# A two-layer gated cross-attention block with a mixture of experts: later token groups summed inside the expert loop, and the first steps of layer 0 issued in another order

## The chip, the cores and the metric

The kernel runs on one core of one Trainium2 chip, in one launch. The metric is the device time of the launch in microseconds. The kernel before takes 2547.64 us, the median of three runs (2542.3 to 2548.95).

## The reference

All tensors are float32. `x` is 32 groups of 112 tokens of 256 numbers; `ctx_512` is 32 contexts of 375 rows of 128. Four residual branches follow each other:

```
x = x + tanh(g_xattn[0]) * L0_xattn(layernorm(x), ctx_512)   # 16 heads of 16
x = x + tanh(g_ffn[0])   * L0_ffn(layernorm(x))              # gated recurrence over the 32 groups
x = x + tanh(g_xattn[1]) * L1_xattn(layernorm(x), ctx_512)   # 16 heads of 64
x = x + tanh(g_ffn[1])   * L1_ffn(layernorm(x))              # experts
```

The last one is the branch that most of the change is about:

```
xf = x.reshape(T, D)                                  # 3584 tokens
shared = silu(xf @ Ws_up) @ Ws_down
aff = xf @ centroids.T
_, idx = jax.lax.top_k(aff + expert_biases, 8)        # 8 of 64 experts
w = sigmoid(take_along_axis(aff, idx, axis=1))
w = w / (sum(w, axis=-1) + 1e-08)
...
y = einsum('etf,efd->etd', silu(einsum('td,edf->etf', xf, W_up)), W_down)
routed = sum over the 8 experts of a token of w * y
return shared + routed
```

## The kernel before

A group is one index `b` of 0 to 31, 112 tokens on 112 partitions. The tiles `xs[0]` to `xs[7]` hold four groups each. The kernel has these stages, by the time of the profile: layer 0's attention (0 to about 580 us), the recurrence and layer 1's attention (to about 1990 us), and the experts (to the end).

**The start of layer 0.** Five queues are filled from the first microsecond. SP's queue loads `cols` (L83), `cent` (the centroids, L129), `rows` (all row constants, spread over 112 partitions, L150), `xs[0]` (L331), `cts[0]` (four contexts, L334), `wv` and `wo`. ACT's queue loads `wk` and `wq` and then computes `tg = tanh(gates)` out of `rows` (L151). GpSimd clears buffers, makes `bias0` out of `rows` and `tg` (L397), and raises the variances to the power of minus one half (L402, L405) for the first normalisation; between these two it halves `sdn`, the shared experts' second matrix (L747). VectorE normalises (L411), TensorE turns the result over (L423) and projects queries (`queries0`, L433) and keys (`keys0`, L450). Each projection is copied to SBUF by ACT and then spread by eight small DMAs: a key tile `k` goes into two tiles `kT` (L457, SP's queue), a query tile `q` into `qp` (L441). Before the loop, the eight DMAs of query half 0 are issued by ACT, those of half 1 by SP. Item `n` of the loop (`n // 4` the group, `n % 4` a set of four heads) needs `kT` of item `n` and one four-head part of `qp`: items 0 and 1 use the two parts of half 0, items 2 and 3 those of half 1. `quad` computes the scores `sc` (L483) and their maxima `nm` (L487); two items later the transposed scores `st` (L498) and their exponentials (L504). The call `keys0(n + 2)` stands in every even item, so that the keys of items 2 and 3 are made in item 0. The order of TensorE, VectorE, ACT and GpSimd is the program's own here (a manual schedule).

**The experts.** Each expert's token rows lie in the DRAM table `xrows`. The function `run` works through pairs `n` of 128-row blocks: pairs 0 to 63 are the first two blocks of each expert, the 68 pairs after them (`NSURE` = 136 blocks) are blocks that an expert has beyond 256 rows, ordered by the group in which the block begins. A pair is loaded by SP (L1126), turned over, multiplied up, through silu, down, and scattered by GpSimd's indirect DMAs into the DRAM table `yrows` (L1212), one row for each of a token's 8 experts. A token's branch is the sum of its 8 rows in `yrows`.

**The sums.** There are three forms.

- `early_sums`, groups 0 to 15 (`NHALF` = 16): inside `run`, a group's rows are loaded in two halves of four rows.
- `late_sums`, groups 16 to 20 (up to `NEARLY` = 21): inside `run` from pair `hi - 4` on, two steps to a group, a group's rows loaded in four quarters of two rows (`yq`, 224 KB each) into the five buffers that the blocks `xblk` use. Step 0 of a group adds the pair of quarters that the former group's step 0 loaded, and loads quarters 0 and 1; step 1 does the same for quarters 2 and 3, joins the two halves and adds the sum to `xs` (`to_x`). A quarter takes the next buffer that an addition frees, so that each load but the first of a group waits for an addition of the group before.
- `sums`, groups 21 to 31: after `run`, a group's 8 rows are loaded whole (`y8`, 896 KB), four buffers, with VectorE (L1341, L1346, L1347) and GpSimd (L1342) adding.

Loads in the first two forms are made by `early`: such a load waits for scatters, but not for the newest six (`2 * LAG`). That is right only if no row of the group is in these; so the kernel counts blocks on the chip: `planned` is 6 blocks for each group, and `late` marks a group by whose end more blocks have begun than planned. If one of the first `NEARLY` groups is marked, the program takes a branch in which `run` makes no sums at all, and `sums(0, NEARLY)` follows. By the reference's routing of these inputs, 0 to 98 blocks have begun by the ends of groups 0 to 27, and 129 by the end of group 31; no group is marked.

Between `run` and `sums` stand three branches that every engine takes, for the two forms of `run` (L1355 to L1357), for blocks beyond the sure ones (L1360) and for `sums(0, NEARLY)` (L1365). Each branch that skips code waits for the queues' semaphores and fetches the instructions behind it. Finished groups go to the output two at a time from ACT's queue (`results_out`, L1326).

Of the kernel before, what the change touches and what calls it, by code (L numbers as in the profile page):

```python
# [33 lines left out]
AF = mybir.ActivationFunctionType  # L34
ALU = mybir.AluOpType
# [4 lines left out]
B, S, D = 32, 112, 256  # L40
# [10 lines left out]

NBLK = 216
SBLK = 2 * E
NEARLY = 21
NHALF = 16
EARLY = 8
LAG = 3
NSURE = 136
# [10 lines left out]
R_BO0, R_BOF, R_BO1, R_EB, R_G = 0, 256, 512, 768, 832  # L69
# [4 lines left out]
def flamingo_kernel(ctx: ExitStack, tc: tile.TileContext, a: dict, out: bass.AP):  # L74
    nc = tc.nc
# [8 lines left out]
    tg = const.tile([S, 4], F32, tag="tg", name="tg")  # L84
# [29 lines left out]
    nc.gpsimd.iota(planned32, [[0, 1]], base=2 * (EARLY - 5 - LAG), channel_multiplier=6)  # L114
    planned = rtp.tile([B, 1], F32, tag="planned", name="planned")
    nc.vector.tensor_copy(planned, planned32)
    place32 = rtp.tile([S, TOPK], I32, tag="place32", name="place32")
    nc.gpsimd.iota(place32, [[1, TOPK]], base=0, channel_multiplier=TOPK)
    place = rtp.tile([S, TOPK], F32, tag="place", name="place")
# [6 lines left out]
    half = rtp.tile([S, G], F32, tag="half", name="half")  # L126
    nc.gpsimd.memset(half, -0.5)
    cent = rtp.tile([128, 2, E], F32, tag="cent", name="cent")
    nc.sync.dma_start(cent, a["centT"].rearrange("(c p) e -> p c e", p=128))  # L129
    dram = ctx.enter_context(tc.tile_pool(name="dram", bufs=1, space=DRAM))  # L130
    xrows = dram.tile([E * NT, PW], F32, tag="xrows", name="xrows")
    yrows = dram.tile([NT * TOPK, D], F32, tag="yrows", name="yrows")
# [1 line left out]
    def disjoint(group, ins):  # L134
# [9 lines left out]
    sdn = rtp.tile([F, D], F32, tag="sdn", name="sdn")  # L144
    nc.gpsimd.dma_start(sdn, a["ws_down"])
    attention = ExitStack()
    rows = attention.enter_context(tc.tile_pool(name="rows", bufs=1)).tile(
        [S, NROW], F32, tag="rows", name="rows"
    )
    nc.sync.dma_start(rows, a["rows"].partition_broadcast(S))  # L150
    nc.scalar.activation(tg, rows[:, R_G : R_G + 4], AF.Tanh)  # L151
    work = attention.enter_context(tc.tile_pool(name="work", bufs=2))


# [155 lines left out]
    with ExitStack() as att:  # L310
# [14 lines left out]
        with ExitStack() as ph:  # L325
# [6 lines left out]
            nc.scalar.dma_start(wk, a["wk0"])  # L332
            nc.scalar.dma_start(wq, a["wq0"].rearrange("(c p) m -> p c m", p=128))
            nc.sync.dma_start(cts[0], a["ctxT"][:, 0:G, :])  # L334
            nc.sync.dma_start(wv, a["wv0"])
            nc.sync.dma_start(wo, a["wo0"].rearrange("(c p) m -> p c m", p=128))


            one = wp.tile([128, 1], F32, tag="one", name="one0")
# [40 lines left out]
            def inputs(n):  # L380


                b, g = n // 4, n % 4
                if n == 1:
                    nc.gpsimd.dma_start(xs[1], a["x"][G : 2 * G].rearrange("b s d -> s b d"))
                if g == 2 and b + G < B:
                    nc.gpsimd.dma_start(
                        cts[b // G + 1][:, b % G, :], a["ctxT"][:, b + G, :]
                    )
                if g == 3 and b + 2 * G < B:  # L390
                    nc.gpsimd.dma_start(xs[b // G + 2][:, b % G, :], a["x"][b + 2 * G])
                if g == 0 and 8 <= b < 24 and b % 2 == 0:
                    nc.gpsimd.dma_start(*halves[b // 2 - 4])
# [32 lines left out]
                    )  # L426
                nc.scalar.copy(xTs[g][:, c, :], pt)

            def queries0(g, i, queue=nc.sync):

                pq = ps_m.tile([128, GT], F32, tag="mm", name=f"pq0_{g}_{i}")
                for k in range(2):
                    nc.tensor.matmul(  # L433
                        pq, wq[:, k, 128 * i : 128 * i + 128], xTs[g][:, k, :],
                        start=(k == 0), stop=(k == 1),
                    )

                q = kvp.tile([128, GT], F32, tag="q", name=f"q0_{g}_{i}")
                nc.scalar.activation(q, pq, AF.Identity, bias=bq4[:, i : i + 1], scale=0.25)
                for h in range(8):  # L440
                    queue.dma_start(  # L441
                        qps[g % 2][h % 4 * 32 : h % 4 * 32 + 16, 2 * i + h // 4, :],
                        q[16 * h : 16 * h + 16, :],
                    )

            def keys0(n):

                b, i = n // 4, n % 4 // 2
                pk = ps_m.tile([128, LKV], F32, tag="mm", name=f"pk0_{n}")
                nc.tensor.matmul(  # L450
                    pk, wk[:, 128 * i : 128 * i + 128], cts[b // G][:, b % G, :],
                    start=True, stop=True,
                )
                k = kvp.tile([128, LKV], F32, tag="k", name=f"k0_{n}")
                nc.scalar.activation(k, pk, AF.Identity, bias=cols[:, C_BK + i : C_BK + i + 1])
                for h in range(8):
                    nc.sync.dma_start(  # L457
                        kTs[(n + h // 4) % 6][h % 4 * 32 : h % 4 * 32 + 16, :],
                        k[16 * h : 16 * h + 16, :],
                    )  # L460
# [120 lines left out]
            for j in range(G):  # L581
                normed0(0, j, nc.vector)
            keys0(0)
            for c in range(2):
                turned0(0, c)
            for i in range(2):
                queries0(0, i, (nc.scalar, nc.sync)[i])


            rest = []  # L590
            for n in range(4 * B + 7):
                b, g = n // 4, n % 4
                ng, turn = b // G + 1, (b % G, g)
                inputs(n)
                if ng < NG and b % G == 2:
                    normed0(ng, g)
                quad(n, (0, 1), n - 2, (2, 3))
                for r in rest:
                    r()
                rest = []  # L600
                if ng < NG and turn == (1, 3):
                    row_stats(ng * G + 2)
                if 0 <= n - 3 < 4 * B:
                    values_of(n - 3)
                if 0 <= n - 1 < 4 * B:
                    with_max(n - 1)
                quad(n, (2, 3), n - 2, (0, 1))
                if ng < NG and b % G == 1 and g != 2:
                    row_stats(ng * G + g)
                    if g == 3:  # L610
                        rstd0(ng)
                if g == 2 and b >= 2:
                    row_stats(b - 2)
                    if (b - 2) % G == G - 1:
                        inverse_std(rstd_r, (b - 2) // G)
                if n % 2 == 0 and n + 2 < 4 * B:
                    keys0(n + 2)
                if b < B and g < NKC:
                    values0(b, g)
                if ng < NG and turn in ((2, 3), (3, 0)):  # L620
                    turned0(ng, (g + 1) % 4)
                if ng < NG and turn in ((3, 1), (3, 2)):
                    queries0(ng, g - 1, nc.gpsimd)
                if g == 3 and b >= 1:
                    rest.append(divided(b - 1))
                elif g == 0 and b >= 2:
                    rest.append(turned_back(b - 2))
                elif g == 1 and b >= 2:
                    rest.append(output0(b - 2))
# [12 lines left out]
        with ExitStack() as ph:  # L642
# [79 lines left out]
            for t in range(B):  # L722
# [6 lines left out]
                h = work.tile([S, D], F32, tag="t", name=f"h_{t}")  # L729
# [11 lines left out]
        with ExitStack() as ph:  # L741
# [2 lines left out]
            ps_s = ph.enter_context(tc.tile_pool(name="ps_s1", bufs=4, space=PSUM))  # L744
            ps_m = ph.enter_context(tc.tile_pool(name="ps_m1", bufs=3, space=PSUM))
            ps_o = ph.enter_context(tc.tile_pool(name="ps_o1", bufs=1, space=PSUM))
            nc.gpsimd.tensor_scalar(sdn, sdn, 0.5, None, ALU.mult)  # L747
            rstd = rstd_1
            xns, xTs, qTs, kTs, vs, ps, pTs, outs, pos = ({} for _ in range(9))
            routing = []  # L750
# [181 lines left out]
            for n in range(N + 3):  # L932
# [14 lines left out]
                h, c = n // 8 + 1, n % 8  # L947
                g, i = n // 16 + 1, n % 16
# [52 lines left out]
    with tc.tile_pool(name="tables", bufs=1) as ep:  # L1001
# [24 lines left out]
        for k, (lhs, rhs) in enumerate((  # L1026
# [19 lines left out]
        nc.tensor.matmul(  # L1046
            pt[:, 1:2], late[:NEARLY], ones[:NEARLY, 0:1], start=True, stop=True
        )
# [223 lines left out]
    def late_sums(t):  # L1272
# [3 lines left out]
        if t >= 2:  # L1276
# [4 lines left out]
            if k:  # L1281
                add(z, live["q", c, 1])
                to_x(c, z)
                if c % 2 and c < NEARLY:
                    results_out(c - 1)
        if b < NEARLY:
            for q in (2 * k, 2 * k + 1):
# [5 lines left out]
    def run(lo, hi, with_sums=False):  # L1293
        with tc.manual_schedule(engines={
            nc.tensor.engine, nc.vector.engine, nc.scalar.engine, nc.sync.engine,
        }):
            for n in range(lo, min(lo + 4, hi)):
                rows_in(n)
            for n in range(lo, hi + 7 + with_sums):
                if n + 4 < hi:  # L1300
                    rows_in(n + 4)
                if n % 8 == 0 and n < 48:
                    weights(2 + n // 8, nc.sync)
                if n < hi:
                    turned(n)
                if lo <= n - 2 < hi:
                    up(n - 2)
                if lo <= n - 4 < hi:
                    if n - 4 < E:
                        down(n - 4)  # L1310
                    else:
                        hidden_turned(n - 4)
                if lo <= n - 6 < hi and E <= n - 6:
                    down(n - 6)
                if with_sums and n >= E + EARLY:
                    early_sums(n - E - EARLY)
                if with_sums and n >= hi - 4:
                    late_sums(n - hi + 4)
# [46 lines left out]
    with tc.If(is_late > 0):  # L1365
        sums(0, NEARLY)
    sums(NEARLY, B)

# [56 lines left out]
```

## Time and profile before

| what | value |
|---|---|
| median of the runs | 2547.64 us (2542.3 to 2548.95) |
| time of the profiled execution | 2544.75 us |
| its span | 2543.0 us |
| busy share of the span: TensorE, VectorE, ACT, GpSimd | 91%, 66%, 47%, 36% |
| first two score matmuls of item 2 of layer 0 | 36.19 us |
| granted TensorE clock, 28 to 44 us | 0.50 |
| last quarter-wise sum ends | 2481.16 us |
| first whole-group load issued, first one added | 2488.12 us, 2495.99 us |
| last whole-group load added | 2535.62 us |

The profile is of one execution. A line of the timeline has the start and the duration in microseconds, the engine (a name with q is an engine's queue: register work, branches, semaphores and DMA issues), the line of the source, the operation with output and inputs, and in brackets how long the engine had been idle and what ended that. A DMA's line is its issue, not its transfer; when it has landed is seen from who waited for it. A line of the window view has, for each stretch, the busy time of the engines, the granted clock, the mean busy share of the 16 DMA engines and what they moved in GB/s.

### The profile page before, as it was taken

Reading aid. Unit: us, or ns where it says so; the run is one execution under the profiler, and the core shown is the slowest. Engines: PE = TensorE matmul, PEld = TensorE weight load, DVE = VectorE, ACT = ScalarE, POOL = GpSimd, SP = SyncE. Lnnn points to the kernel's source line nnn. Section 1 sums busy time; section 2 is a strip of 40 time slices with the busy share of each in tenths; the row PEclk is TensorE's granted clock in tenths of the full one; section 3 lists DMA queues with packets and bytes.
Section 4 is the critical chain, followed back from the end, with each engine's and each line's share of the span. In section 5 each row is a group of like instructions: output and inputs, shape, how many; then the busy total and the mean of one; then the engine's idle time right before and its main releaser. Section 6 shows DMA issues by size and latency. Waiting matters only on the chain. (4 is left out here: it accounts for less than half of the span.)

```text
span 2543.0 us, 64448 instructions
## 1 busy us (share of the span) xinstructions
PE 2303.5 (91%) x24199; PEld 1811.8 (71%) x24199; DVE 1685.7 (66%) x5075; ACT 1190.8 (47%) x3156; POOL 910.0 (36%) x1149
## 2 busy tenths in 40 slices
PE   7999999999999999999999999999999487888860
PEld 4777777778996777777777777777777366666640
DVE  5666666764327778777777877777777544455565
ACT  2555555543334555555555555555555143344430
POOL 3333333201000034333334443443344466655552
PEclk8999999999999999999999999999999698899985
DMA  3122211116300000000000000000101687567777
GB/s 84 50 57 64 60 49 50 38 34 223 118 1 1 2 26 29 27 29 27 29 29 30 29 29 29 29 28 27 31 29 33 204 277 236 166 201 223 207 202 182
DMA packets 144313, 204.56 MB, mean 80 GB/s; under 512 B 26168, under 2 KB 120970, under 8 KB 143985
## 3 DMA queue, kind: packets, MB, share of 16 engines
q1 hardware_dynamic: 101040, 99.80, 14.0%
q0 software_dynamic: 36352, 94.05, 11.4%
q10 hardware_dynamic: 6592, 6.39, 0.8%
q8 instruction: 199, 3.26, 0.5%
q14 instruction: 130, 1.06, 0.1%
HBM read 100.67 MB, written 88.74 MB: 74 GB/s over the span
## 5 line engine op out<-in xcount | busy, mean ns | idle before, releaser
L301 POOL DMA_INDIRECT xrows<-row,at x256 | 256.1, 1001 | 530.0 <-DVE at L298 340.3
L841 ACT ACTIVATE p_a<-ps_a,nmax_a 112x375 f32<-112x375 f32 x512 | 286.2, 571 | 232.2 <-DVE nmax_a L840 156.5
L487 DVE TENSOR_REDUCE nm<-sc 112x1 f32<-112x375 f32 x512 | 256.7, 543 | 182.5 <-PE st L498 138.5
L1212 POOL DMA_INDIRECT yrows<-yblk,dst x264 | 261.7, 991 | 208.5 <-ACT yblk L1200 121.0
L504 ACT ACTIVATE pT<-st 125x336 f32<-125x336 f32 x512 | 202.7, 448 | 252.8 <-PE st L498 252.8
L865 PEld LDWEIGHTS pt_a<-ident,p_a 112*125 112x125 f32 x1536 | 224.4, 188 | 78.7 <-ACT v L819 19.2
L840 DVE TENSOR_REDUCE nmax_a<-ps_a 112x1 f32<-112x375 f32 x512 | 244.4, 539 | 20.0 <-PE ps_a L836 17.2
L483 PE MATMUL sc<-kT,qp 32*112 32x375 f32 x1024 | 233.3, 526 | 3.1 <-DMA qp<-q 1.8
L498 PE MATMUL st<-qa,kT 32*125 32x112 f32 x3072 | 234.8, 284 | 0.0
L865 PE MATMUL pt_a<-ident,p_a 112*125 112x112 f32 x1536 | 228.3, 271 | 0.6 <-ACT kT L801 0.6
L812 PE MATMUL pv<-wv,c 128*125 128x256 f32 x768 | 216.3, 391 | 10.3 <-ACT kT L801 6.2
L797 PE MATMUL pk<-c,wk 128*128 128x375 f32 x512 | 208.0, 488 | 4.1
L890 PEld LDWEIGHTS pav<-pT_a,v 64*64 64x64 f32 (+1 forms) x6144 | 171.2, 133 | 45.8 <-issue 44.5
L498 PEld LDWEIGHTS st<-qa,kT 32*125 32x125 f32 x3072 | 189.0, 184 | 3.3 <-DVE nm L487 0.4
L836 PE MATMUL ps_a<-kT,qT 64*48 64x375 f32 (+1 forms) x2048 | 190.3, 486 | 0.0
L890 PE MATMUL pav<-pT_a,v 64*64 64x112 f32 (+1 forms) x6144 | 182.4, 257 | 2.0 <-issue 1.9
L853 DVE TENSOR_SCALAR p_a<-p_a,inv_a 112x375 f32<-112x375 f32 x512 | 177.7, 410 | 4.5
L801 ACT COPY kT<-pk 128x375 f32<-128x375 f32 x256 | 120.8, 472 | 106.5 <-PE pk L797 101.5
L872 DVE COPY pT_a<-pt_a 125x448 f32<-125x448 f32 x128 | 78.9, 616 | 106.0 <-PE pt_a L865 106.0
L812 PEld LDWEIGHTS pv<-wv,c 128*125 128x125 f32 x768 | 124.4, 188 | 29.4 <-ACT kT L801 21.6
L1179 DVE SCALAR_TENSOR_TENSOR h<-h,ph 128x256 f32<-128x256 f32 x132 | 55.0, 417 | 134.2 <-ACT h L1178 118.5
L908 PE MATMUL po_a<-wo,oT 128*112 128x256 f32 x512 | 143.1, 402 | 0.0
(276 smaller groups left out, 4579.9 us busy)
## 6 DMA issues: line engine op xcount, KB each, us to landing
xblk<-xrows SPq DMA_DIRECT2D x136, 140.0 KB
xrows<-blank POOLq DMA_DIRECT2D x2, 8960.0 KB
xblk<-xrows SPq DMA_DIRECT2D x64, 280.0 KB
y<-yrows SPq DMA_DIRECT2D x32, 448.0 KB
kT<-k SPq DMA_DIRECT2D x512, 23.4 KB
y<-yrows SPq DMA_DIRECT2D x11, 896.0 KB
wall<-in_w_up SPq DMA_DIRECT2D x7, 1024.0 KB
wall<-in_w_down SPq DMA_DIRECT2D x7, 1024.0 KB
```

Source lines behind the costliest of these rows:

```text
L301: disjoint("xrows", nc.gpsimd.indirect_dma_start(out=xrows[:, :], out_offset=bass.IndirectOffsetOnAxis(ap=at[:, k : k + 1], axis=0), in_=r ...
L483: nc.tensor.matmul(sc, qps[b // G % 2][32 * j : 32 * j + 32, g, j0 : j0 + S], kTs[n % 6][32 * j : 32 * j + 32, :], start=True, stop=True,)
L487: nc.vector.tensor_reduce(nms[n % 3][:, j, 16:17], sc, AX.X, ALU.max, negate=True)
L498: nc.tensor.matmul(st[j][:, kc, :], kTs[m % 6][32 * j : 32 * j + 32, kc * KC : (kc + 1) * KC], qas[m][32 * j : 32 * j + 32, :], start=True ...
L504: nc.scalar.activation(pTs[m][:, j], st[j], AF.Exp)
L797: nc.tensor.matmul(pk, wk[:, c * 128 : (c + 1) * 128], cts[b // G][:, b % G, :], start=True, stop=True,)
L812: nc.tensor.matmul(pv[:, i, :], ct[:, (lo + i) * KC : (lo + i + 1) * KC], wv[:, g * 256 : (g + 1) * 256], start=True, stop=True,)
L840: nc.vector.tensor_reduce(nmax[:, j : j + 1], sc, AX.X, ALU.max, negate=True)
L841: nc.scalar.activation(p[:, j, :], sc, AF.Exp, bias=nmax[:, j : j + 1], accum_out=tot[:, j : j + 1],)
L865: nc.tensor.transpose(pt[:, j * S : (j + 1) * S], p[:, j, kc * KC : (kc + 1) * KC], ident[:S, :S],)
L890: nc.tensor.matmul(po[q][64 * r : 64 * r + 64, i, :], v[k0:k1, kc, 64 * j : 64 * j + 64], pT[k0:k1, kc, j * S : (j + 1) * S], start=(kc == ...
L1212: scatter = nc.gpsimd.indirect_dma_start(out=yrows[:, :], out_offset=bass.IndirectOffsetOnAxis(ap=dst[:, i : i + 1], axis=0), in_=y[:, i, ...
```

## The change

`NEARLY` becomes 28: groups 21 to 27 are now summed in quarters by `late_sums` inside `run`, and `sums` is left with groups 28 to 31. The loop of `run` gets as many empty steps at its end as that needs. `planned` is cut at `NSURE - 2 * LAG` = 130 blocks. At the start, `rows` and `tg` come after the first context, `cent` after `wo`; the keys of items 2 and 3 are made before the first queries; each query half's eight DMAs are split, four from SP and four from GpSimd, none from ACT; and `sdn` is halved at item 8 of layer 0.

```diff
-NEARLY = 21
+NEARLY = 28
...
     nc.vector.tensor_copy(planned, planned32)
+    nc.vector.tensor_scalar(planned, planned, float(NSURE - 2 * LAG), None, ALU.min)
...
-    nc.sync.dma_start(cent, a["centT"].rearrange("(c p) e -> p c e", p=128))
...
-    nc.sync.dma_start(rows, a["rows"].partition_broadcast(S))
-    nc.scalar.activation(tg, rows[:, R_G : R_G + 4], AF.Tanh)
...
             nc.sync.dma_start(cts[0], a["ctxT"][:, 0:G, :])
+            nc.sync.dma_start(rows, a["rows"].partition_broadcast(S))
+            nc.scalar.activation(tg, rows[:, R_G : R_G + 4], AF.Tanh)
             nc.sync.dma_start(wv, a["wv0"])
             nc.sync.dma_start(wo, a["wo0"].rearrange("(c p) m -> p c m", p=128))
+            nc.sync.dma_start(cent, a["centT"].rearrange("(c p) e -> p c e", p=128))
...
+                if n == 8:
+                    nc.gpsimd.tensor_scalar(sdn, sdn, 0.5, None, ALU.mult)
...
-            def queries0(g, i, queue=nc.sync):
+            def queries0(g, i, *queues):
...
                 for h in range(8):
-                    queue.dma_start(
+                    queues[h * len(queues) // 8].dma_start(
...
             keys0(0)
+            keys0(2)
             for c in range(2):
                 turned0(0, c)
             for i in range(2):
-                queries0(0, i, (nc.scalar, nc.sync)[i])
+                queries0(0, i, nc.sync, nc.gpsimd)
...
-                if n % 2 == 0 and n + 2 < 4 * B:
+                if n % 2 == 0 and 0 < n < 4 * B - 2:
                     keys0(n + 2)
...
-            nc.gpsimd.tensor_scalar(sdn, sdn, 0.5, None, ALU.mult)
...
-            for n in range(lo, hi + 7 + with_sums):
+            for n in range(lo, max(hi + 7, with_sums * (hi - 2 + 2 * (NEARLY - NHALF)))):
```

## The prediction

> **What bounds the kernel now.** I read the chain of waits first, then the timeline of the end (VectorE, then SP), the waits of SP's queue, and for the start the timeline and the windows.
>
> ```profile
> DMA y<-yrows 1%; DVE x L1347 0%; DVE y L1341 0%; DVE y L1346 0%; SPq L1322 0%
> ...
> 2472.30 0.30 SPq L1322 DMA_DIRECT2D yq<-yrows  x1
> 2474.48 1.58 SPq L1322 DMA_DIRECT2D yq<-yrows  x2
> 2488.12 39.34 SPq L1322 DMA_DIRECT2D y<-yrows  x11
> ...
> 2473.77 1.41 DVE L1241 TENSOR_TENSOR yq<-yq,yq 112x512 f32<-112x512 f32 x2
> 2478.77 1.42 DVE L1241 TENSOR_TENSOR yq<-yq,yq 112x512 f32<-112x512 f32 x2 [0.54 <-DMA yq<-yrows]
> 2480.68 0.48 DVE L1246 SCALAR_TENSOR_TENSOR x<-yq,tg,x 112x256 f32<-112x256 f32 x1
> 2495.99 1.23 DVE L1341 TENSOR_TENSOR y<-y 112x1024 f32<-112x1024 f32 x1 [14.82 <-DMA y<-yrows]
> 2507.29 1.23 DVE L1341 TENSOR_TENSOR y<-y 112x1024 f32<-112x1024 f32 x1 [0.65 <-DMA y<-yrows]
> 2535.62 1.22 DVE L1341 TENSOR_TENSOR y<-y 112x1024 f32<-112x1024 f32 x1 [0.63 <-DMA y<-yrows]
> ...
> 2476.19 63.61 ACTq L1326 DMA_DIRECT2D out<-x  x8
> ...
> SPq L1357 <- SPq L1357: 4.6, 2, 3.4
> ...
> 2479.00:2482.00 3.00, 0.00 (x0) 0.00 (x0) 2.06 (x4) 0.00 (x0) 0.00 (x0) 0.50 0.12 37
> 2500.00:2504.00 4.00, 0.00 (x0) 0.00 (x0) 2.75 (x4) 0.00 (x0) 1.38 (x1) 0.50 1.12 236
> ```
>
> The chain ends in the whole-group loads: from 2488.12 nothing counts but the transfer of `yrows`. Eleven groups are added from 2495.99 to 2535.62: 39.63 / 10 = 3.96 us each, with the DMA engines full (share 1.12 in the last line). Before that the quarter-wise sums run until 2480.68 + 0.48 = 2481.16, and 6.96 us pass at the branches. The two steps-1 of the last quarter-wise groups begin at 2473.77 and 2478.77: 5.00 us apart, against 3.96, and the DMA share falls to 0.12 behind them: these small loads are paced by waiting, not by bytes.
>
> ```profile
> 10.40 0.97 POOL L397 TENSOR_SCALAR bias<-rows,tg 112x256 f32<-112x256 f32 x1
> 13.06 1.98 POOL L747 TENSOR_SCALAR sdn<-sdn 128x256 f32<-128x256 f32 x1
> 13.94 5.03 SPq L457 DMA_DIRECT2D kT<-k  x8
> 15.01 1.05 POOL L405 TENSOR_TENSOR rs<-rs,half 112x4 f32<-112x4 f32 x1
> 23.52 5.07 ACTq L441 DMA_DIRECT2D qp<-q  x8
> 28.64 0.63 ACT L439 ACTIVATE q<-pq,bq 128x448 f32<-128x448 f32 x1 [5.19 <-DMA qp<-q]
> 36.19 1.67 PE L483 MATMUL sc<-kT,qp 32*112 32x375 f32 x2 [0.45 <-DMA kT<-k]
> ...
> 60.00:100.00 40.00, 40.00 (x593) 30.71 (x589) 26.06 (x71) 20.26 (x50) 18.25 (x29) 1.00 0.19 48
> ```
>
> At the start `sdn` stands for 1.98 us between the two steps of `rs`; ACT's own issues keep its second query back 5.19 us; item 2's scores begin at 36.19. From 60 to 100 us TensorE is busy in all 40.00 us at clock 1.00, so a shift of its stream before that reaches the end undiminished.
>
> **The end, part by part.**
>
> *Removed.* Seven of eleven whole groups. With four left, the sums' first loads stand as now and the last is the fourth: 2535.62 - 2507.29 = 28.3 us less.
>
> *Added.* Seven groups in quarters, after group 20. VectorE alone would need 0.7 + 1.42 + 0.42 + 0.48 = 3.0 us a group, so the loads set the pace. In step 1 quarter 2 of the next group is issued after the first addition, quarter 3 after the second (2474.48 and 0.72 later, behind 2473.77 and its 1.41), and the next step 1 begins when quarter 3 has landed: 1.4 us of additions, then 3.6 us from issue to use, 5.0 in all. Step 0 has one addition (0.7) and one such load, and is shorter. Nothing else is queued behind SP's waiting loads by then; the blocks' loads are over. Bounds: 3.96 us a group (the same bytes at the whole groups' pace, where the 16 DMA engines are full) and 7.8 us (VectorE's timeline has the step 0 of group 16 at 2449.65 and of group 17 at 2457.43, with blocks and scatters beside them). I take 4.8: nearest is 5.0, and in that row the last scatters and both output writes of 2476.19 still shared the engines. 7 x 4.8 = 33.6 us more.
>
> The rule that speaks against this is in the Trainium skill, "DMA: Bandwidth & Descriptors", section "Bandwidth": batch transfers to 1 MiB or more. By the fit in its "Anatomy of one DMA" (2.0 us + bytes / 436 GB/s, given for GpSimd's path) a quarter would take 2.5 us, a group 3.9, and the seven 27.5 us, an estimate; the sum of the end would then be +2.7 instead of +8.8. The trace's 3.6 us decides.
>
> *The gap at the branches.* SP waits at L1357 twice, 4.6 us together: 3.4 us for code, and 1.2 more, until the output writes issued at 2476.19 have landed; from there to 2488.12 it is 7.1 us. Before, the last output write ahead of the branches is issued about 5 us before the sums end; with groups 26 and 27 summed last, their write starts only when the sums end. It needs 3 to 4.5 us (the write of about 2476.55 lets SP go at about 2481.1), then the 7.1 follow: 3.0 to 4.6 us more than 6.96. Below, nothing; I take 3.5.
>
> *Sum of the end:* 33.6 + 3.5 - 28.3 = +8.8 us. Bounds: 27.7 + 0 - 28.3 = -0.6, and 54.6 + 4.6 - 28.3 = +30.9.
>
> The cut of `planned` is one small VectorE operation (its neighbours take 0.13 to 0.40 us) among constants, hidden by the 1.3 us for which VectorE waits for `rs` at 16.10; uncovered it would cost those 0.2 us.
>
> **The start, part by part.**
>
> *Loads.* Ahead of `cts[0]` there are now 64 + 366 KB less of 1,635. TensorE's first key product waits for it until 11.71; at some 250 KB/us it comes 1.7 us earlier, and SP's first key DMA at about 12.2 instead of 13.94. `rows` lands where `cts[0]` did, about 11.4, so `bias0` moves from 10.40 to 11.6 and the first step of `rs` is behind it at 12.6; without `sdn` the power (1.05) follows that step (0.6) at once, and the normalised `x` starts near 14.3 instead of 16.10.
>
> *Queues.* SP issues sixteen key DMAs now, 0.63 us each: 12.2 + 10.1 = 22.3. The first query (ready at 23.45, now 21.7) waits for that: SP's first query DMA goes out at 22.3 against ACT's 23.52, 1.2 us earlier. GpSimd issues its four beside it (0.55 us each, as its loads of 20.33 to 22.01) and is free from 17.8. ACT's second query no longer waits 5.19 us. The four and four that GpSimd issues stand ahead of its loads of `xs[1]` and of contexts, which come some 5 us later; the first of these is used in item 4, after 43 us. The halving of `sdn`, 0.4 to 2 us of GpSimd at item 8, is far from its use in layer 1.
>
> *TensorE.* The key product of 1.62 us at 28.69 leaves the place between items 0 and 1, and item 2 no longer waits 0.45 us for `kT`: 1.2 + 1.6 + 0.45 = 3.3 us. The granted clock is 0.50 from 28 to 44 us, full from 46; a denser stream may bring it up sooner: items 2 and 3 begin 6.9 us apart (36.19, 43.07), two later ones about 4, so up to 3 us more. I take -3.5; bounds -1.2 and -7. If item 1 waits for GpSimd's slower landings (its first load was issued at 19.51, and 22 to 24 moves 302 GB/s), the lower gain holds.
>
> **Sum:** +8.8 - 3.5 = +5.3 on the profiled 2544.75 (span 2543.0): 2550. The median of the runs is 2.9 higher: **2553**.
>
> **The rivals.** About 0.3% (7.6 us) is what a measurement tells from no change.
>
> *Slow quarters (0.30).* The quarters stay as slow as beside the scatters: 6 us a group (the steps 0 at 2471.59 and 2477.54). 42 + 3.5 - 28.3 - 3.5 = +13.7: 2561. From 5.13 us a group on it is slower than 0.3%. For it: late landings are what each step waits for, and the output writes remain. Against: the scatters are over (124 GB/s from 2473 to 2476, 37 from 2479).
>
> *Hidden sums (0.14).* With the scatters gone the quarters reach 3.96 us, and the clock rises early: 27.7 + 3.5 - 28.3 - 7 = -4.1: 2543.5; and if the gap does not grow either, -7.6: 2540, the edge of what counts as faster. For it: the DMA share of 0.12 behind 2479. Against: each load's wait for an addition.
>
> *The other branch (0.01).* Were a group marked late, 32 whole groups would follow `run`: 21 x 3.96 = +83 us, 2631. The routing (98 of 130 blocks by group 27) speaks against it.
>
> *Forecast (0.55):* 4.3 to 5.1 us a group, -2 to -6 at the start; own range 2545 to 2557.
>
> The chances: faster 0.10 (of the hidden sums); slower 0.27 of the slow quarters, 0.05 of the forecast, 0.01 of the branch: 0.33; the same 0.57. The range, 2542 to 2562, reaches to both rivals.
>
> **What would show it.** Seven more steps 1 of quarter-wise sums, 4.8 us apart; the first whole-group load some 10 us after the last sum; four whole groups 3.5 to 4.2 us apart; item 2's scores near 33 us; `sdn` gone from the first 20 us. Wrong it would be if these steps came under 4.2 or over 5.2 us apart, if item 1 waited for GpSimd's queue, or if a load in the sums waited for a scatter.

## The result, and the profile after

| | before | after |
|---|---|---|
| median of 7 runs each | 2547.64 us (2539.74 to 2552.97) | 2554.78 us (2551.88 to 2556.86) |
| ratio to before, 95% interval | | 1.0029 [1.0016, 1.0042] |
| span of the profiled execution | 2543.0 us | 2550.2 us |
| last step 1 of group 20 begins | 2478.77 us | 2479.01 us |
| last quarter-wise sum ends | 2481.16 us | 2516.72 us |
| first whole-group load issued | 2488.12 us | 2525.71 us |
| last whole-group load added | 2535.62 us | 2542.67 us |
| first score matmuls of item 2, layer 0 | 36.19 us | 33.72 us |

The change costs 0.29% (0.16 to 0.42), some 7 us. The prediction was 2553. The chain that ended last in the changed kernel still ends in the whole groups' loads:

```profile
DMA y<-yrows 1%; SPq L1325 0%; DVE x L1350 0%; DVE y L1344 0%; DVE y L1349 0%
```

Its timeline of the end (VectorE and SP). The lines "x2" are the steps 1 of groups 20, 21, 26 and 27, those of L1344 the first and the last of the four whole groups:

```profile
2479.01 1.42 DVE L1244 TENSOR_TENSOR yq<-yq,yq 112x512 f32<-112x512 f32 x2 [0.84 <-DMA yq<-yrows]
2484.35 1.42 DVE L1244 TENSOR_TENSOR yq<-yq,yq 112x512 f32<-112x512 f32 x2 [1.03 <-DMA yq<-yrows]
...
2509.93 1.42 DVE L1244 TENSOR_TENSOR yq<-yq,yq 112x512 f32<-112x512 f32 x2 [1.61 <-DMA yq<-yrows]
2514.32 1.42 DVE L1244 TENSOR_TENSOR yq<-yq,yq 112x512 f32<-112x512 f32 x2 [1.40 <-DMA yq<-yrows]
...
2532.63 1.22 DVE L1344 TENSOR_TENSOR y<-y 112x1024 f32<-112x1024 f32 x1 [15.91 <-DMA y<-yrows]
2542.67 1.22 DVE L1344 TENSOR_TENSOR y<-y 112x1024 f32<-112x1024 f32 x1 [0.27 <-DMA y<-yrows]
...
2525.71 5.37 SPq L1325 DMA_DIRECT2D y<-yrows  x4
```

And the waits of its SP queue between 2478 and 2526 us (total, times, longest):

```profile
SPq L1325 <- DVE yq L1244: 18.7, 21, 2.3
SPq L1360 <- SPq L1360: 7.8, 3, 4.3
SPq L1325 <- DVE x L1249: 3.6, 6, 0.7
SPq L1363 <- SPq L1363: 3.3, 1, 3.3
```

From 2479.01 to 2514.32 are seven groups: 35.31 / 7 = 5.04 us each. Every step 1 waits for a load, and SP, which issues that load, waits 21 times for an addition (18.7 us) and 6 times for the last step of a sum (L1249, 3.6 us): each side waits for the other. The lines of L1360 and L1363 are waits at the branches. The DMA engines meanwhile are not full; the window view shows it (busy times by engine, granted clock, DMA share, GB/s):

```profile
2485.00:2490.00 5.00, 0.00 (x0) 0.00 (x0) 2.92 (x6) 0.00 (x0) 0.00 (x0) 0.50 0.66 178
2495.00:2500.00 5.00, 0.00 (x0) 0.00 (x0) 2.54 (x5) 0.00 (x0) 0.00 (x0) 0.50 0.55 154
```

These are two of the seven windows of 5 us from 2480 to 2515 us; over the seven the share is 0.50 to 0.85 and 0.67 in the mean, six tenths of the 1.12 that the whole groups had in the kernel before (in this view a share can come out above 1). And the start, lines picked from the same kernel's timeline:

```profile
3.20 7.27 DVE L345 TENSOR_SCALAR bq<-cols 128x2 f32<-128x2 f32 x1 [2.23 <-DMA cols<-in_cols]
6.91 3.57 DVE L155 BATCH_NORM_STATS2 bn<-x 112x6 f32<-112x256 f32 x1
10.05 0.39 POOL L366 MEMSET nm<- 112x128 f32 x2
11.57 0.93 POOL L400 TENSOR_SCALAR bias<-rows,tg 112x256 f32<-112x256 f32 x1 [1.12 <-ACT tg L334]
12.49 0.70 POOL L405 TENSOR_SCALAR rs<-stats 112x4 f32<-112x4 f32 x1
13.54 1.38 POOL L215 TENSOR_SCALAR row<-place 112x8 f32<-112x8 f32 x1 [0.35 <-DVE place L121]
14.89 1.05 POOL L408 TENSOR_TENSOR rs<-rs,half 112x4 f32<-112x4 f32 x1
15.98 2.20 DVE L414 TENSOR_SCALAR xn_a<-x,stats,rs 112x256 f32<-112x256 f32 x4 [1.17 <-POOL rs L408]
```

`sdn` is gone from between the two steps of `rs`, but another step stands there now: `row<-place`, which belongs to layer 1 and had run behind the power before (0.24 us at 16.06). It waits for a copy on VectorE and takes 1.38 us beside the copies that follow there. The power starts at 14.89 against 15.01: nothing gained. VectorE's two first lines, a step on 128x2 elements that "takes" 7.27 us and the first statistics that take 3.57, both end at 10.47 us, when GpSimd's fills end (10.05 + 0.39 = 10.44).

Between the two profiled executions layer 0's item 2 is 2.5 us earlier, layer 1's last softmax 3.05 us (1963.04 and 1959.99). In the experts the two drift: the first scatter is 0.5 us earlier, one half-way 3.2 us, the last 0.9 us later, and group 20's sum 0.24 us later. One pair of executions, whose runs spread over some 10 us, can't tell whether that is chance. Nor is one execution exact at the start: in the nine kernels below that keep this order of GpSimd's fills, the changed one among them, item 2's scores begin between 32.78 and 35.13 us.

### The profile page after: what moved, and what is told of

Read it like the earlier page. It is cut to its first block, busy times and chain, and to the rows that moved or that the text cites. A ratio compares the mean times of both kernels' runs of the same rounds, so it can differ in the third digit from the quotient of the medians.

```text
span 2550.2 us, 64510 instructions
## 1 busy us (share of the span) xinstructions
PE 2306.6 (90%) x24199; PEld 1812.7 (71%) x24199; DVE 1687.1 (66%) x5090; ACT 1191.6 (47%) x3156; POOL 904.6 (35%) x1150
## 5 line engine op out<-in xcount | busy, mean ns | idle before, releaser
L868 PEld LDWEIGHTS pt_a<-ident,p_a 112*125 112x125 f32 x1536 | 224.3, 188 | 78.8 <-ACT v L822 19.2
L873 ACT COPY pT_a<-pt_a 125x448 f32<-125x448 f32 x256 | 136.6, 534 | 4.6 <-PE pt_a L868 4.1
```

Of the source, the lines that this page charges most:

```text
L868: nc.tensor.transpose(pt[:, j * S : (j + 1) * S], p[:, j, kc * KC : (kc + 1) * KC], ident[:S, :S],)
```

## The experiments

Kernels measured together shared a chip with runs of the kernel before. That took 2434 us on some chips and 2537 to 2548 on others, so times are compared as ratios to it (95% intervals), and otherwise stretches within one trace. Where no ratio is given, the reading rests on the trace of one execution.

### One half of the change at a time

The start alone is the kernel after with `NEARLY` at 21, `planned` not cut and the old loop; the late part alone is the kernel before with these three as in the change.

```diff
-NEARLY = 28
+NEARLY = 21
...
-    nc.vector.tensor_scalar(planned, planned, float(NSURE - 2 * LAG), None, ALU.min)
```

> Only the start of the change; the late part as in the kernel before. Theory (the start's gain is kept to the end): about 3 us less than the kernel before (2544.6 if that reads 2547.6; ratio 0.9988), with item 2's scores near 33.7 us and about 3 us earlier through the routing. Rival (the gain is swallowed where DMA bounds the experts): within 0.8 us of the kernel before, with the landmarks earlier by 3 us up to the routing and by nothing at the last group.

Measured: 0.9987 [0.9973, 1.0], that is -3.2 us (-6.6 to 0). Item 2's scores began at 34.67 us. This is the theory's size, though the interval reaches to nothing and so does not exclude the rival.

> Only the late part of the change; the start as in the kernel before. Theory (the two parts add up): 7 to 10 us more than the kernel before (ratio 1.003 to 1.004): seven quarter groups at 5.0 us, a gap of 9 us, four whole groups in 17 us. Rival (the start's gain was lost in the experts, so the late part alone already costs what the whole change costs): 5 to 7 us more, the same as the whole change within 1 us.

Measured: 1.0049 [1.0035, 1.0064], +11.9 us (+8.5 to +15.6); steps 1 of the quarter sums from 2369.70 to 2404.60, 34.90 / 7 = 4.99 us apart. The gap is 8.84 us, and the four whole groups take 17.15 us from the first issue to the last addition. The interval holds the upper half of the theory's 7 to 10 us, and the rival's 5 to 7 lie below it. -3.2 + 11.9 = 8.7, beside the 7 of the whole change: the parts add up within their intervals.

Two things weaken this. The whole change was timed on another chip, and there the eleven whole groups took 47.50 us, against 44.97 in the run of the start alone: from group 20's last step to the end the change costs 9.2 us between the two traces of this chip and 6.9 between those of the first. And that the start's gain lasts to the end is not shown. On this chip the whole change, with its output held as in a run below, came to 1.0026 [1.0015, 1.0037], less than the late part alone, as the theory wants, but the intervals just touch. In the traces the lead over the late part alone varies: at group 20's sum the start alone is 2.7 us ahead of it, but the run with more buffers (also with the new start) is 0.6 behind and the one with its output held 2.4 behind, though the three were 3.3, 1.2 and 2.1 us ahead at layer 1's last softmax.

### Do the quarter loads wait for buffers, or are small loads slow?

For groups 21 to 27 the second half of the quarters goes into `y0` and `y1`, the four-row tiles that `early_sums` no longer needs. Same bytes, same transfers, nine quarter buffers instead of five.

```diff
+                if k and b > 20:
+                    if q == 2:
+                        pair = ep.tile([S, 4, D + 8], F32, tag=f"y{b % 2}", name=f"yp_{b}", bufs=1)[:, :, :D]
+                    y = live["q", b, q] = pair[:, 2 * q - 4 : 2 * q - 2]
+                else:
```

> The changed kernel, but for groups 21 to 27 the second half of each group's quarters goes into two tiles of four rows that are free by then, so nine quarter buffers stand where five stood; the transfers keep their size (2 rows of each token, 224 KB). Theory (the loads wait until an addition frees a buffer): 3.6 to 4.2 us per group in place of 5.04, so 6 to 10 us less than the changed kernel, and DMA near 1.0 busy there. Rival (transfers of this size are slow in themselves, at 180 to 250 GB/s): 4.9 to 5.1 us per group, within 1.5 us of the changed kernel, and DMA's busy share stays at 0.58 to 0.75.

Measured: 1.0007 [0.9997, 1.0018], against 1.0026 [1.0015, 1.0037] for the next experiment, which has the five buffers: 4.6 us less by the ratios and 6.9 by the medians (2435.16 and 2442.07), where the theory gave 6 to 10. VectorE's timeline of this kernel for groups 22 and 23:

```profile
2378.55 0.68 DVE L1244 TENSOR_TENSOR yq<-yq,yq 112x512 f32<-112x512 f32 x1
2379.32 0.69 DVE L1244 TENSOR_TENSOR yp<-yp 112x512 f32<-112x512 f32 x1
2381.66 0.69 DVE L1244 TENSOR_TENSOR yq<-yq,yq 112x512 f32<-112x512 f32 x1
2383.63 0.69 DVE L1244 TENSOR_TENSOR yp<-yp 112x512 f32<-112x512 f32 x1 [1.27 <-DMA yp<-yrows]
```

Its SP queue's waits between 2372 and 2400 us, and then two of its windows:

```profile
SPq L1332 <- DVE x L1249: 9.6, 5, 2.5
SPq L1332 <- DVE yq L1244: 0.8, 1, 0.8
```

```profile
2382.00:2387.00 5.00, 0.00 (x0) 0.00 (x0) 3.25 (x6) 0.00 (x0) 0.00 (x0) 0.50 1.10 286
2387.00:2392.00 5.00, 0.00 (x0) 0.00 (x0) 3.88 (x7) 0.00 (x0) 0.00 (x0) 0.50 0.94 276
```

From the last step of group 20 (2372.16) to that of group 27 (2400.26) are 28.10 / 7 = 4.01 us a group, where the late part alone took 4.99 on the same chip. That makes 6.8 us over the seven (34.90 - 28.10). Group 22 finds all its loads landed (no bracket behind its lines). The same 224 KB transfers now keep the DMA engines nearly full (0.76 to 1.10 in the five windows from 2372 to 2397 us, 0.96 in the mean, against 0.62 to 0.72 in the late part alone): they were not slow, they were issued late. SP still waits 9.6 us for additions, but with loads in flight. This is shown: the number of buffers set the pace.

### What lengthened the gap at the branches?

Four kernels on one question. First the output rows of groups 26 and 27 are written behind the branches:

```diff
-                if c % 2 and c < NEARLY:
+                if c % 2 and c < NEARLY - 1:
                     results_out(c - 1)
...
+    results_out(NEARLY - 2)
     sums(NEARLY, B)
```

> The changed kernel, but the output rows of groups 26 and 27 are written behind the branches instead of ahead of them. Theory (the branches wait for the newest output write, so the later write of the change lengthened the gap from 6.96 to 8.99 us): the gap falls to about 7 us and the time by about 2 us. Rival (the gap is the engines' own branch steps, which wait for no transfer): gap 8.5 to 9.2 us, time within 1 us.

Measured: 1.0026 [1.0015, 1.0037]; gap 9.13 us. The theory, which was that of my prediction, falls by its number. The records of the branch instructions then showed that VectorE's third jump, over the fallback sums, takes 2.3 us where it had taken 0.2 before. So the fallback was cut to as many groups as before, and then to eight:

```diff
-        sums(0, NEARLY)
+        sums(7, NEARLY)
```

The second of these has `sums(20, NEARLY)` there.

> The changed kernel, but the fallback that is jumped over at the end sums groups 7 to 27 only (21 groups' code as in the kernel before; the fallback, which these inputs do not take, leaves out groups 0 to 6). Theory (VectorE's third jump costs 2.3 us with 28 groups' code behind it and 0.2 with 21): the jump takes 0.2 us and the gap from the last sum to the first load of a whole group is 6.8 to 7.3 us in place of 9.0. Rival (the two us come from the longer run of quarter groups ahead of the jumps): the gap stays at 8.7 to 9.3.

Measured: gap 8.70 us, jump 2.30 us: again the rival's number.

> The changed kernel, but the fallback that is jumped over sums groups 20 to 27 only (8 groups' code; the fallback, which these inputs do not take, leaves out groups 0 to 19). Theory (a jump is cheap where its target lies within code that is already loaded, in pieces of 8 KB): VectorE's third jump takes 0.2 us and the gap falls to about 7 us. Rival (the length of the code jumped over is not what sets it): 2.3 us again, gap about 9.

Measured: the jump takes 0.21 us, as the theory says, and the gap is 8.68 us, as the rival says. That names the missing half: something else ends at nearly the same time. Both edits together:

> The changed kernel with both edits of the earlier runs at once: the output rows of groups 26 and 27 written behind the branches, and the fallback cut to groups 20 to 27 (it leaves out groups 0 to 19). Theory (two chains of jumps of almost the same length end the gap, VectorE's with its long third jump and SP's, which waits for ACT's output write, so that taking away either alone gains 0.3 us or nothing): both together bring the gap from 9.0 to between 6.8 and 7.5 us. Rival (something else holds the first load, such as the waits on SP itself): 8.5 us or more.

Measured: 6.83 us. The timeline of that kernel:

```profile
2405.49 0.48 DVE L1249 SCALAR_TENSOR_TENSOR x<-yq,tg,x 112x256 f32<-112x256 f32 x1
2412.69 0.34 ACTq L1329 DMA_DIRECT2D out<-x  x1
2412.80 5.54 SPq L1325 DMA_DIRECT2D y<-yrows  x4
```

The table reads the branch records of each trace, in us from the end of the last quarter-wise sum. SP has steps of its own behind its third jump (0.93 us in the row of 8 groups, where SP comes last), and VectorE's end must come too; the first load follows the later of the two.

| kernel | VectorE's third jump takes | VectorE behind it | SP behind its third | first load |
|---|---|---|---|---|
| before | 0.21 | 6.80 | 5.88 | 6.96 |
| after | 2.31 | 8.84 | 7.76 | 9.00 |
| output held | 2.57 | 8.98 | 4.54 | 9.13 |
| fallback of 21 groups | 2.30 | 8.55 | 7.29 | 8.70 |
| fallback of 8 groups | 0.21 | 6.76 | 7.75 | 8.68 |
| output held, 8 groups | 0.22 | 6.68 | 4.41 | 6.83 |

So two chains grew by about two us each, VectorE's by its jump and SP's because it waits for ACT, which issues the output write first; take away either and the other still holds the load. Shown by the two rows with one edit and the row with both: all eight traces with four whole groups and without both edits have gaps of 8.68 to 9.13 us. One thing goes the other way. SP's second jump begins 3.3 us later in the changed kernel (3.62 against 0.32 us behind the last sum), but SP's own third jump takes 0.2 us in every kernel that sums 28 groups early, also over 8 groups' code, where it took 2.1 in the kernel before and 1.9 in the start alone; that is why only 1.9 of the 3.3 us are left in SP's column. Why the jump over 21 groups' code is dear in one kernel and cheap in the kernel before stays open; where the code lies was not varied. The Trainium skill, "Runtime: NRT & Kernel Launch", section "Instruction fetch mechanics", says that a taken jump whose target lies outside the two pages of code that are present has to wait until the target's page is loaded. By that, position would count as well as length, which no run here tried. The traces agree so far: single loads of 8 KB on the instruction queue lie between the jumps, and VectorE's jumps take either 0.2 or 2.3 to 3.3 us, nothing between.

### Who holds the start?

`place` is copied in item 8 instead of ahead of everything, so `row<-place` cannot stand before the power:

```diff
-    nc.vector.tensor_copy(place, place32)
...
                 if n == 8:
+                    nc.vector.tensor_copy(place, place32)
```

> The changed kernel, but VectorE's copy that makes the tile 'place' is issued in layer 0's item 8, so GpSimd's first 'row<-place' step, which waits for it, cannot stand between the two halves of 1/std. Theory (that step took the place of the moved 'sdn' step and its cover for the 1.8 us I had forecast): the power starts at 13.2 to 13.6 us in place of 14.9, the first normalised rows at 14.3 to 14.7 in place of 15.98, and item 2's scores 0.5 to 1.5 us earlier. Rival (the normalised rows are held by the clock or by VectorE's other copies): first normalised rows within 0.3 us of 15.98.

Measured: `row<-place` is gone from there, but the power starts at 14.70 and the first normalised rows at 15.79. The lines of this kernel's timeline of GpSimd:

```profile
13.08 1.03 POOL L400 TENSOR_SCALAR bias<-rows,tg 112x256 f32<-112x256 f32 x1 [2.62 <-ACT tg L333]
14.10 0.52 POOL L405 TENSOR_SCALAR rs<-stats 112x4 f32<-112x4 f32 x1
14.70 1.05 POOL L408 TENSOR_TENSOR rs<-rs,half 112x4 f32<-112x4 f32 x1
```

In this execution `rows`, and so `bias0`, came 1.5 us later than in the changed kernel, and the power 1.62 us behind it. But the kernel with the fallback of 21 groups, which still has `row<-place` there, had `bias0` at 13.19 and the power 1.58 us behind: with rows as late as that the step costs nothing. Over the nine kernels with this order of fills `bias0` began between 11.38 and 13.19 us, the normalised rows always between 15.79 and 16.31. So the run is inconclusive on `row<-place` (the theory's 14.3 to 14.7 was not reached, and 15.79 is the rival's number, within 0.3 us of 15.98): the step and the rows end at about the same time, now the one last and now the other.

The fills of `v` and `nm` moved behind `1/std` on GpSimd:

```diff
-                nc.gpsimd.memset(v, 0.0)
-                nc.gpsimd.memset(v[:, :, :, 16:17], 1.0)
...
-                nc.gpsimd.memset(nm, 0.0)
...
             rstd0(0)
+            for nm in nms:
+                nc.gpsimd.memset(nm, 0.0)
             for j in range(G):
                 normed0(0, j, nc.vector)
+            for v in vs:
+                nc.gpsimd.memset(v, 0.0)
+                nc.gpsimd.memset(v[:, :, :, 16:17], 1.0)
```

> The changed kernel, but GpSimd's fills of the two v tiles come behind the addition of bias0 and those of the three nm tiles behind 1/std, so that its fills end at about 7.2 us in place of 10.4. Theory (VectorE's first steps last as long as GpSimd's fills run): VectorE's first statistics end near 7.5 us in place of 10.47, and the four statistics by 9.5 in place of 12.5; 1/std still waits for the rows and the 'row<-place' step, so the first normalised rows come 1 to 3 us earlier. Rival (VectorE waits for x or for its code): the first statistics still end at 10 us or later.

The timeline of VectorE and GpSimd in that kernel:

```profile
3.24 3.99 DVE L345 TENSOR_SCALAR bq<-cols 128x2 f32<-128x2 f32 x1 [2.27 <-DMA cols<-in_cols]
4.05 3.15 POOL L353 MEMSET qp<- 128x1792 f32 x2
7.90 0.43 DVE L155 BATCH_NORM_STATS2 bn<-x 112x6 f32<-112x256 f32 x1 [0.68 <-DMA x<-in_x]
13.09 0.93 POOL L397 TENSOR_SCALAR bias<-rows,tg 112x256 f32<-112x256 f32 x1 [5.90 <-ACT tg L334]
```

VectorE's small step ends at 7.23 with the last of the two fills that are left (7.20), and the first statistics take 0.43 us instead of 3.57: that the fills hold VectorE is shown. The normalised rows came only at 15.51, 0.5 us earlier where the theory gave 1 to 3, since GpSimd's queue has `bias0`, which waits for `rows`, ahead of `1/std`.

### A version that beats both

All 32 groups are summed by quarters inside the first branch, with the nine buffers, and all that needs another path stands in one other branch. The bound of 130 blocks then holds for all groups; these inputs have 129, so another routing would take the slow branch.

```diff
-NEARLY = 28
+NEARLY = 32
...
     with tc.If(is_late > 0):
         run(0, sure)
-    found = nc.values_load(n_blk[0:1, 0:1], min_val=0, max_val=NBLK)
-    with tc.If(found > NSURE):
-        run(sure, (SBLK + NBLK) // 2)
-    moe.close()
-    with tc.If(is_late > 0):
-        sums(0, NEARLY)
-    sums(NEARLY, B)
+        found = nc.values_load(n_blk[0:1, 0:1], min_val=0, max_val=NBLK)
+        with tc.If(found > NSURE):
+            run(sure, (SBLK + NBLK) // 2)
+        sums(0, B)
+    moe.close()
```

> All 32 groups summed by quarters inside the first branch (second halves in the two four-row tiles from group 21 on), and everything that needs all blocks put into one other branch, so no jump lies between the sums and none ahead of the last loads; the start as in the changed kernel. Theory (nine buffers give 4.0 us per group and the gap is the jumps): eleven groups behind the last block in 44 us in place of the kernel before's 58, one jump of 3 us at the end beside the last output's write; with the start's 3 us some 14 to 17 us less than the kernel before. Rival (quarter groups are slow without the whole groups' depth, or the jump at the end costs what the gap cost): 3 to 8 us less than the kernel before.

Measured: 0.9936 [0.9922, 0.995], -16.2 us (-19.8 to -12.7). Two windows of it, then the last step of its last group on the timeline:

```profile
2480.00:2490.00 10.00, 0.00 (x0) 0.00 (x0) 7.03 (x13) 0.00 (x0) 0.00 (x0) 0.50 0.95 278
2490.00:2500.00 10.00, 0.00 (x0) 0.00 (x0) 8.59 (x15) 0.00 (x0) 0.00 (x0) 0.50 0.97 268
```

```profile
2514.06 0.48 DVE L1249 SCALAR_TENSOR_TENSOR x<-yp,tg,x 112x256 f32<-112x256 f32 x1
```

Eleven groups behind group 20 take 43.5 us (3.96 each, DMA engines full), where the kernel before takes 58.3 for its gap and eleven whole groups. The span ends at 2519.3, 4.8 us behind the last sum against 3.6 before: the one jump left costs 1.2 us beside the last write.

To that, a start without the three things found above: VectorE fills `nm` and `v`, `bias0` and the tanh come behind the first queries, `place` in item 8, and item 2's keys behind the queries on SP.

```diff
-            keys0(0)
-            keys0(2)
+            for z in nms + vs:
+                nc.vector.memset(z, 0.0)
+            keys0(0)
...
                 queries0(0, i, nc.sync, nc.gpsimd)
+            keys0(2)
+            nc.scalar.activation(tg, rows[:, R_G : R_G + 4], AF.Tanh)
+            nc.gpsimd.tensor_scalar(bias0, rows[:, R_BO0 : R_BO0 + D], tg[:, 0:1], None, ALU.mult)
```

> The kernel with one branch (all groups by quarters), and a start in which VectorE instead of GpSimd fills the nm and v tiles (behind the normalised rows), the tanh of the gates, bias0 and its additions come behind the first queries, item 2's keys behind the queries on SP, and 'place' is copied in item 8. Theory (the start is held by GpSimd's fills and by 1/std standing behind the rows): first normalised rows at 11 to 13 us in place of 16, first scores at 21 to 23.5 in place of 25.5, item 2's scores at 30 to 32 in place of 33.7, and another 2 to 4 us, so 18 to 20 us less than the kernel before. Rival (the start is then held by the slow clock or by SP's key transfers): item 2's scores not before 33 us and the same time as without the new start, 15 to 17 us less.

Measured: 0.9913 [0.9898, 0.9927], -21.2 us (-24.8 to -17.8), 5 us beyond the version without this start; the two intervals overlap. The timeline of its start:

```profile
9.14 0.79 POOL L400 TENSOR_SCALAR rs<-stats 112x4 f32<-112x4 f32 x1 [1.94 <-DVE one L339]
10.02 1.51 POOL L403 TENSOR_TENSOR rs<-rs,half 112x4 f32<-112x4 f32 x1
11.56 1.38 DVE L413 TENSOR_SCALAR xn_a<-x,stats,rs 112x256 f32<-112x256 f32 x4
20.16 2.75 PE L486 MATMUL sc<-kT,qp 32*112 32x375 f32 x8 [0.33 <-DMA qp<-q]
27.11 0.97 PE L486 MATMUL sc<-kT,qp 32*112 32x375 f32 x2
```

The normalised rows come at 11.56 instead of 15.98, item 2's scores at 27.11 instead of 33.72 (better than the theory's 30 to 32), and the lead stands in layer 0's middle (6.5 us ahead of the changed kernel). Several covers lay over one another: the two edits tried alone were worth 0.2 and 0.5 us at the normalised rows, all together 4.4. `bias0` behind `1/std` was not tried alone, nor this start without the one branch.

## Why the prediction was right, and where not

| term | predicted | measured |
|---|---|---|
| seven quarter groups | +33.6 (4.8 each) | +35.3 (5.04 each) |
| gap at the branches | +3.5 | +2.0 |
| whole groups (eleven before, four after) | -28.3 | 47.50 before, 16.96 after: -30.5 |
| start, at item 2 | -3.5 | -2.5 |
| start, at the end | -3.5 | -3.2 (-6.6 to 0) in the run of its own; +0.24 at group 20 in the profiled pair |
| sum | +5.3 | +7.1 by the medians; 35.3 + 2.0 - 30.5 + 0.24 = +7.0 in the profiled pair |

The main step held: quarters beside five buffers are paced by additions and late loads, not by bytes, and seven of them cost more than the seven whole groups that they replace. The row of 5.0 us between two steps 1 in the kernel before was the right one; I took 4.8 because scatters and output writes shared that row, and those had not been its cause: the scatters were over, output writes went on every two groups, and the mean was 5.04. The experiment with nine buffers shows why the bound of 3.96 was not reached, and that it nearly is (4.01) as soon as loads may run ahead; the rival of hidden sums needed four more buffers, not less traffic. Slow quarters at 6 us did not come (single spacings of two steps 1 were 4.39 to 5.87, three of the seven above the 5.2 that was to be a sign of error), nor the other branch: 28 groups were summed early. That the sum came within 2 us of the measured one is partly luck: its terms were off by +1.7, -1.5, -2.2 and, in the profiled pair, +3.7 us, and much of that cancelled.

The four whole groups were cheaper than a cut of the old row: 6.92 us from the first issue to the first addition, and 10.04 for the next three, against 7.87 and 11.30. Between additions they were 3.2 to 3.5 us apart, where 3.5 to 4.2 had been forecast. I left them "as now". In the nine kernels with four such groups they took 16.0 to 17.8 us, the first four of eleven 17.9 and 19.2, though issued at the same spacing; why stays open. With the gap it is why the end came to +6.8 instead of +8.8, though the quarters were dearer.

The gap's mechanism was half of the truth. It said that the late output write holds SP for 3 us. Held back, it freed SP by 3.2 us (7.76 to 4.54), as forecast; but the load did not come earlier, since a jump that I had not looked at had become as long. The step that failed is "from there to 2488.12 it is 7.1 us", a length taken as fixed. From SP's second jump to the first load it was 6.6 us before and 5.4 after: SP's third jump had become 1.9 us shorter, VectorE's 2.1 longer, and the load followed VectorE.

At the start the step that failed is "without `sdn` the power (1.05) follows that step (0.6) at once, and the normalised `x` starts near 14.3". In its place stood `row<-place`, and 15.98 was measured; the later rows of other executions would have held it as long. I had only looked at what left. That `cts[0]` lands earlier held (first key product 9.76 instead of 11.71), SP's sixteen key issues too (12.81, 10.10 us), and the first query DMA at 23.01 came 0.5 us before ACT's 23.52 where I had forecast 1.2; item 2's gain was 2.5 of 3.3. The granted clock rose from 0.50 to 1.00 at 41.8 us instead of 44.7, about as far as the stream had moved (item 3 begins at 40.34 instead of 43.07), so the 3 us more that the range allowed for did not come. The gain was 1.6 us at layer 0's last exponentials (583.25 and 581.66) and 3.05 at the end of layer 1. The prediction read from TensorE, full between 60 and 100 us, that a lead reaches the end undiminished. That reading does not cover the experts, where TensorE was busy for only 79 to 82 of 100 us (2100 to 2300 us, kernel before): there the profiled lead was gone (group 20's sum came 0.24 us later), and the runs do not settle whether it always is.

## What to carry to other kernels

Where two engines take turns at a small pool of buffers, the spacing of their steps is set by the buffers and not by the size of the transfers: look at the DMA share between the steps, and if it is well below that of larger loads (0.67 against 1.12 here), add buffers before judging the transfer size. When something is removed from between two steps, look up in the new order what slides into the place, and what the second-latest cover is: the two waits at the branches were worth 0.3 us or nothing one by one and 2.2 together, and of the start's, two tried alone were worth 0.2 and 0.5 us at the normalised rows, against 4.4 for all. And before code is moved across a branch, price the jumps: doing the rest of the work inside the branch that is taken, with the nine buffers, gained 16 us where the change itself cost 7.

## What the runs showed of the hardware

A row of fills on GpSimd holds VectorE's first steps until it ends: 7.27 us for a step on 2 elements a partition with 6.4 us of fills beside it, 3.99 with 3.15. The Trainium skill, "SBUF — State Buffer", section "Who interferes with whom", says that in VectorE's two-port modes the two engines share a pair of ports, which the first to issue keeps for its whole instruction while the other waits. Here the wait spans the whole row of fills; in which mode VectorE's step ran no run shows.

A taken jump took 0.2 us or 2.3 to 3.3 us on VectorE; the code jumped over plays a part (with 8 groups of it instead of 28 the third jump fell from 2.3 to 0.2 us), but its length alone does not decide: over 21 groups' code the jump took 0.2 us in the kernel before and 2.3 in the changed one, and on SP it took 2.1 us in the kernel before and 0.2 in every kernel with 28 groups summed early.

The same kernel before took 2434 us on three chips and 2537 to 2548 in the other two series of runs. Most of the difference lies in the experts: from the first scatter to the last it took 358 us in the run of the start alone and 451 us in the profile before, at DMA rates of 244 to 331 against 191 to 281 GB/s (2040 to 2300 us). The granted clock differs little over the span (0.972 and 0.962). Why was not tried.
